# A graph network on one core: where batch norm stands in the first batch of three convolutions

## The chip, the cores and the metric

The kernel runs on one core of one Trainium2 chip. The metric is the device time of one execution in microseconds, lower is better; runs are given by their median. Besides the plain runs there is one profiled execution, whose trace all durations are taken from. The engines are called PE (TensorE, matmuls), DVE (VectorE), ACT (ScalarE), POOL (GpSimd) and SP (SyncE, here a queue for DMAs).

## What is computed

There are 16 graphs (batches) of 1024 nodes with 128 features each, and a symmetric 0/1 adjacency matrix of 1024 x 1024 for every graph. A gated recurrent graph network of four layers comes first. Then four graph convolutions follow, and the change concerns these. Cut to what matters, the reference of the second part is:

```python
h = jnp.maximum(_layernorm(x, axis=-1), 0.0)
for i in range(4):
    h = jnp.einsum('bnm,bmc->bnc', adj, h @ W[i]) + b[i]
    h = jax.nn.relu(h)
    mu = jnp.mean(h, axis=(0, 1))
    var = jnp.mean(jnp.square(h - mu), axis=(0, 1))
    h = gamma[i] * (h - mu) * jax.lax.rsqrt(var + EPS) + beta[i]
return x + h
```

The mean and the variance of batch norm are taken over all nodes of all 16 graphs, so no value of the next layer's input is known before the last graph of this layer is done. Batch norm is one scale and one shift for each feature channel.

In the kernel features lie in the partitions (128) and nodes along the free axis. The last line of a layer is then `h * scale + shift`, with scale and shift of shape 128 x 1.

## The kernel before

There are two paths. `general_path` runs only if a flag shows inputs that a shorter number format can't hold; here it doesn't run. All that follows is in `exact_path`.

The recurrent part (to line 854) writes to DRAM, for each batch, the transposed adjacency matrix in bfloat16 (`adjT_d`), the layer's result (`xmid_d`) and the normed input of the convolutions (`ymid_d`). Its weights are in `w_mT` and `w_hhT`.

The four convolutions (lines 864 to 990) go through the batches one by one. In what follows convolution 1 is the first, with i = 0 in the code, and convolutions 2 to 4 have i = 1 to 3.

- `load_adjT(b, i)` (line 868) loads the eight row blocks of a batch's adjacency matrix from DRAM, 256 KB each, through SP's queue. They land in eight single tiles (`packed`, even batches) or one large tile (`block`, odd batches). ACT (line 876, every third one) or DVE (line 878) widens each to a 128 x 1024 tile `wide`. The tag `row` has twelve buffers: eight for the batch in work and four for the next.
- `conv_input(b, i, aff)` (line 895) applies scale and shift to the features `feat[b]` on ACT (line 897).
- `conv_hw(b, i, hT)` (line 900) multiplies by W on PE (line 493). The product of one batch is split by `features_times` into two parts, a rounded one (ACT, line 495) and the rest (DVE, line 496), so that the fast matmul format loses nothing.
- `aggregate` (line 511) multiplies the adjacency rows by these two parts: for each of eight row blocks j two parts and two halves of the nodes, 32 matmuls of 128 x 512 a batch (line 516), accumulated in two PSUM banks. The banks are `m0`, `m1` in even batches and `g_r`, `g_z` in odd ones (`banks`, line 906). The last batch of convolutions 2 to 4 uses `aggregate_apart` (line 503), which does one half of the nodes after the other.
- `conv_done` (line 909) applies ReLU and the bias on ACT (line 912), puts the result in `feat[b]`, and takes its statistics on DVE (line 913).
- `affine(i, stats)` (line 882) makes scale and shift: one aggregation of the statistics on DVE (885), a square root on ACT (888), and four small DVE operations (889 to 892).

In convolution 1 there is no batch norm in front. There the kernel aggregates first (`first_split`, line 916, splits the input) and multiplies by W behind it: `first_weights` (line 924) copies the two PSUM halves to SBUF and multiplies by W in `g_hn`, `g_xn` (line 931). It does that for batch b in the middle of the aggregation of batch b+1, and for the last batch after everything else.

In convolutions 2 to 4 the product with W of batch b+1 is written ahead of the aggregation of batch b. Batch 0's normalization and product stand ahead of the loop over batches, and so behind the last batch of the layer before:

```python
    for i in range(1, L):
        stats = small.tile([P, B * NH, 6], F32, tag="bn_st", name=f"stats{i}")
        hw = conv_hw(0, i, conv_input(0, i, aff))
        for b in range(B):
            rows = load_adjT(b, i)
            hw_next = conv_hw(b + 1, i, conv_input(b + 1, i, aff)) if b + 1 < B else None
```

After the fourth convolution the result is scaled and shifted, turned back, added to `xmid_d`'s values and written (lines 993 to 1004).

In the recurrent part the order of some or all queues is written out by hand (`manual_schedule`). In the convolutions it isn't: the framework makes each engine's order when the program is built, from the order of the source and its own estimate of when operands are ready. On the chip each engine then runs its own instructions in that fixed order, and waits for the others through semaphores.

Of the kernel before, what the change touches and what calls it, by code (L numbers as in the profile page):

```python
# [8 lines left out]
F32 = mybir.dt.float32  # L9
F32R = mybir.dt.float32r  # L10
# [3 lines left out]
AF = mybir.ActivationFunctionType  # L14
ALU = mybir.AluOpType
AX = mybir.AxisListType
P = 128
HALF = 512
# [323 lines left out]
def exact_path(  # L342
# [21 lines left out]
    nc = tc.nc  # L364
    B, N, C = x.shape
    L = g_weight.shape[0]
    NB = N // P
    NH = N // HALF
    BH = HALF // P
# [9 lines left out]
    def acc(tag, name):  # L379
        return ps_m.tile([P, HALF], F32, tag=tag, name=name)  # L380

    def tmp(name):
        return ps_t.tile([P, HALF], F32, tag="tmp", name=name)
# [8 lines left out]
    def row_tile(name):  # L392
        return keep.tile([P, N], F32R, tag="row", name=name, bufs=12)

    def half_tile(name):
        return keep.tile([P, N], BF16, tag="half", name=name, bufs=8)

    def turned_tile(name):
        return keep.tile([P, NB, N], BF16, tag="adjT", name=name, bufs=1)

    def hw_tiles(b, name):
        return [keep.tile([P, N], F32R, tag=f"hw{b % 2}{s}", name=f"{name}_{s}") for s in range(2)]
# [6 lines left out]
    ones = const.tile([P, 1], F32, tag="ones", name="ones")  # L409
# [3 lines left out]
    w_c = const.tile([P, L, C], F32, tag="w_c", name="w_c")  # L413
    w_mT = const.tile([P, L, 3 * C], F32, tag="w_mT", name="w_mT")
# [12 lines left out]
    def cvec(kind, i):  # L427
        o = 6 * L + kind * L + i
        return vecs[:, o : o + 1]
# [54 lines left out]
    def features_times(w, hT, hw, g, name):  # L484

        pt = tmp(f"hw_{name}_{g}")
        for q in range(BH):
            j = g * BH + q
            src = hT[:, j * P : (j + 1) * P]
            if w is None:  # L490
                nc.tensor.transpose(pt[:, q * P : (q + 1) * P], src, ident)  # L491
            else:
                nc.tensor.matmul(pt[:, q * P : (q + 1) * P], src, w, start=True, stop=True)  # L493
        cols = slice(g * HALF, (g + 1) * HALF)
        nc.scalar.copy(hw[0][:, cols], pt)  # L495
        nc.vector.tensor_sub(hw[1][:, cols], pt, hw[0][:, cols].bitcast(F32))  # L496

    def aggregate_apart(pm, hw, rows):

        for hf in range(NH):  # L500
            for j in range(NB):
                for s in range(2):
                    nc.tensor.matmul(  # L503
                        pm[hf],
                        hw[s][:, j * P : (j + 1) * P],
                        rows[j][:, hf * HALF : (hf + 1) * HALF],
                        start=(j == 0 and s == 0),
                        stop=(j == NB - 1 and s == 1),
                    )

    def aggregate(pm, hw, rows, g):
        for q in range(BH):
            j = g * BH + q
            for s in range(2):
                for hf in range(NH):
                    nc.tensor.matmul(  # L516
                        pm[hf],
                        hw[s][:, j * P : (j + 1) * P],
                        rows[j][:, hf * HALF : (hf + 1) * HALF],
                        start=(j == 0 and s == 0),  # L520
                        stop=(j == NB - 1 and s == 1),
                    )


    with ExitStack() as st:
        work = st.enter_context(tc.tile_pool(name="work", bufs=2))
# [338 lines left out]
    work = ctx.enter_context(tc.tile_pool(name="work2", bufs=2))  # L865
    feat = [feat_pool.tile([P, N], F32, tag=f"f{b}", name=f"feat{b}") for b in range(B)]

    def load_adjT(b, i):
        ts = []
        block = turned_tile(f"block{b}_{i}") if b % 2 else None  # L870
        for j in range(NB):
            t = block[:, j, :] if b % 2 else half_tile(f"packed{b}_{i}_{j}")
            nc.sync.dma_start(t, adjT_d[b][:, j, :])
            r = row_tile(f"wide{b}_{i}_{j}")
            if j % 3 == 1:
                nc.scalar.copy(r, t)  # L876
            else:
                nc.vector.tensor_copy(r, t)  # L878
            ts.append(r)
        return ts  # L880

    def affine(i, stats):

        mv = small.tile([P, 2], F32, tag="bn_mv", name=f"bn_mv{i}")
        nc.vector.bn_aggr(mv, stats.rearrange("p k s -> p (k s)"))
        sc = small.tile([P, 1], F32, tag="bn_sc", name=f"bn_sc{i}")
        sh = small.tile([P, 1], F32, tag="bn_sh", name=f"bn_sh{i}")
        nc.scalar.activation(sc, mv[:, 1:2], AF.Sqrt, bias=eps_t)
        nc.vector.reciprocal(sc, sc)
        nc.vector.tensor_mul(sc, sc, cvec(1, i))  # L890
        nc.vector.tensor_mul(sh, mv[:, 0:1], sc)
        nc.vector.tensor_sub(sh, cvec(2, i), sh)
        return sc, sh

    def conv_input(b, i, aff):
        hT = work.tile([P, N], F32, tag="h", name=f"bn{b}_{i}", bufs=3)
        nc.scalar.activation(hT, feat[b], AF.Identity, bias=aff[1], scale=aff[0])
        return hT

    def conv_hw(b, i, hT):  # L900
        hw = hw_tiles(b, f"chw{b}_{i}")
        for g in range(NH):
            features_times(w_c[:, i, :], hT, hw, g, f"c{b}_{i}")
        return hw

    def banks(b, i):
        return [acc(t, f"pc{b}_{i}_{t}") for t in (("m0", "m1") if b % 2 == 0 else ("g_r", "g_z"))]

    def conv_done(b, i, pm, stats):
        for hf in range(NH):  # L910
            dst = feat[b][:, hf * HALF : (hf + 1) * HALF]
            last = nc.scalar.activation(dst, pm[hf], AF.Relu, bias=cvec(0, i))
            nc.vector.bn_stats(stats[:, b * NH + hf, :], dst)
        return last

    def first_split(b):
        yt = flat(f"y{b}").rearrange("p k c -> p (k c)")
        nc.gpsimd.dma_start(yt, ymid_d[b])
        hw = hw_tiles(b, f"chw{b}_0")
        nc.scalar.copy(hw[0], yt)  # L920
        nc.vector.tensor_sub(hw[1], yt, hw[0].bitcast(F32))
        return hw

    def first_weights(b, pm, stats):

        mt = work.tile([P, N], F32, tag="h", name=f"cm{b}", bufs=3)
        pc = [acc(t, f"pw{b}_{t}") for t in ("g_hn", "g_xn")]
        for hf in range(NH):
            cols = slice(hf * HALF, (hf + 1) * HALF)
            nc.scalar.copy(mt[:, cols], pm[hf])  # L930
            nc.tensor.matmul(pc[hf], w_c[:, 0, :], mt[:, cols], start=True, stop=True)  # L931
        return conv_done(b, 0, pc, stats)

    xo = []

    def by_node(d, hf):
        return d.rearrange("(k p) c -> p k c", p=P)[:, hf * BH : (hf + 1) * BH, :]

    def fetch_x(b):
# [13 lines left out]
        for k in range(0 if b == 2 else 4, len(xo)):  # L953
            for hf in range(NH):
                nc.gpsimd.dma_start(xo[k][hf].rearrange("p (k c) -> p k c", c=C), by_node(xmid_d[k], hf))

    stats = small.tile([P, B * NH, 6], F32, tag="bn_st", name="stats0")
    hw, waiting = first_split(0), None
    for b in range(B):
        rows = load_adjT(b, 0)  # L960
        hw_next = first_split(b + 1) if b + 1 < B else None
        pm = banks(b, 0)
        aggregate(pm, hw, rows, 0)
        if waiting:
            last = first_weights(*waiting, stats)
            if b == 1:
                with tc.issue_after(last.ins):
                    sb.rest()
        aggregate(pm, hw, rows, 1)
        hw, waiting = hw_next, (b, pm)  # L970
    first_weights(*waiting, stats)
    aff = affine(0, stats)

    for i in range(1, L):
        stats = small.tile([P, B * NH, 6], F32, tag="bn_st", name=f"stats{i}")
        hw = conv_hw(0, i, conv_input(0, i, aff))
        for b in range(B):
            rows = load_adjT(b, i)
            hw_next = conv_hw(b + 1, i, conv_input(b + 1, i, aff)) if b + 1 < B else None
            if i == L - 1:  # L980
                fetch_x(b)
            pm = banks(b, i)
            if b + 1 < B:
                for g in range(NH):
                    aggregate(pm, hw, rows, g)
            else:
                aggregate_apart(pm, hw, rows)
            conv_done(b, i, pm, stats)
            hw = hw_next
        aff = affine(i, stats)  # L990


    turns = ["tmp", "tmp", "m0", "m1", "g_r", "g_z", "g_hn", "g_xn"]
    for b in range(B):
        hT = conv_input(b, L, aff)
        for hf in range(NH):
            tag = turns[(b * NH + hf) % len(turns)]
            pt = tmp(f"pt_o{b}_{hf}") if tag == "tmp" else acc(tag, f"pt_o{b}_{hf}")
            for q in range(BH):
                k = hf * BH + q  # L1000
# [56 lines left out]
```

## Time and profile before

| what | value |
|---|---|
| median of 3 runs | 1886.74 us (1886.47 to 1887.95) |
| profiled execution, its own time | 1884.96 us |
| span of its trace (first to last instruction) | 1883.2 us |
| mean granted PE clock | 0.986 |
| aggregation in the recurrent part (line 516, `pm`) | 2048 matmuls, 403 ns each |
| aggregation in even batches of the convolutions (line 516, `pc_m`) | 1024 matmuls, 396 ns each |
| h·W of convolutions 2 to 4 (line 493) | 768 instructions, 286 ns each |
| normalization of 128 x 1024 (line 897) | 64, 1239 ns each |
| widening of one row block | DVE 160 + 160, 693 ns; ACT 96 + 96, 1048 ns |
| load of one row block, issue to landing | 5.3 to 5.7 us (median) |

How to read it. Times are in microseconds from the first instruction of the trace. Matmuls are pipelined, so one of 396 ns doesn't hold the engine for as long; the distance between the starts of two is the time that it costs. `PEld` is the load of the weights, which runs beside the matmuls. An fp32 matmul on `w_c` appears as two instructions in the trace. A row such as `[5.07 <-ACT bn L897]` says that the engine stood idle for 5.07 us before this instruction and that what ended the idleness was an operation `bn` of ACT, line 897. The clock is given as a share of full speed.

### The profile page before, as it was taken

How to read it: one execution, taken by the hardware profiler on the slowest of the kernel's cores; microseconds unless marked ns; L12 is line 12 of the kernel's file. 1: busy time of each engine (PE TensorE's matmuls, PEld its weight loads, DVE VectorE, ACT ScalarE, POOL GpSimd, SP SyncE). 2: the span in 40 equal slices, each digit the busy share in tenths (PEclk: the TensorE clock that was granted, in tenths of full speed). 3: DMA queues.
4: the chain of work that ended last, by engine and by line, in shares of the span. 5: the costliest groups of instructions: out<-in, count | busy, mean ns of one | idle time of the engine just before them, and what ended most of it. 6: DMA issues, size and time to landing. Idle time of an engine off the chain costs nothing.

```text
span 1883.2 us, 21902 instructions
## 1 busy us (share of the span) xinstructions
PE 1826.3 (97%) x7324; PEld 1259.9 (67%) x7324; DVE 1209.0 (64%) x2235; ACT 1041.8 (55%) x1561; POOL 287.5 (15%) x369
## 2 busy tenths in 40 slices
PE   7999999999999999999999999999989989989995
PEld 4666656666656566656665666667768878878884
DVE  5746864865784685595586476576656656665664
ACT  4354563563545454445456353476767767767764
POOL 3130230231141032033023012010100000000021
PEclk8999999999999999999999999999999999999997
DMA  7487476385386476557547536269956757675768
GB/s 258 120 229 255 157 203 216 140 223 170 134 256 189 147 190 202 200 168 234 190 157 203 208 114 169 85 220 319 305 187 214 246 179 246 223 247 180 250 208 259
DMA packets 267824, 381.21 MB, mean 202 GB/s; under 512 B 149716, under 2 KB 171896, under 8 KB 263864
## 3 DMA queue, kind: packets, MB, share of 16 engines
q1 hardware_dynamic: 250032, 246.21, 43.2%
q0 software_dynamic: 17456, 133.45, 20.2%
q8 instruction: 59, 0.97, 0.2%
q14 instruction: 61, 0.50, 0.1%
q10 hardware_dynamic: 216, 0.08, 0.0%
HBM read 287.39 MB, written 117.44 MB: 215 GB/s over the span
## 4 chain that ended last, share of the span: by engine, by line
PE 44%; issue 5%; DMA 3%; DVE 2%; POOL 1%; ACT 1%; SPq 0%; DVEq 0%; POOLq 0%; ACTq 0%
PE pc_m L516 12%; PE pc_g_r L516 5%; PE pc_g_z L516 5%; PE pm L516 5%; PE hw_c L493 5%; PE g_z L720 2%; PE g_r L720 2%; DMA adjT<-half 2%; PE g_xn L720 1%; PE g_hn L720 1%; PE pt_o L1001 1%; PE pw_g_hn L931 1%; PE pw_g_xn L931 1%; PE pc_g_r L503 1%; PE hw_g L491 0%
## 5 line engine op out<-in xcount | busy, mean ns | idle before, releaser
L516 PE MATMUL pm<-row,ghw 128*128 128x512 f32 x2048 | 505.0, 403 | 1.7 <-ACT ghw L697 1.7
L516 PEld LDWEIGHTS pm<-row,ghw 128*128 128x128 f32 x2048 | 383.4, 188 | 107.0 <-issue 31.6
L516 PE MATMUL pc_m<-wide,chw 128*128 128x512 f32 x1024 | 247.6, 396 | 0.0
L516 PEld LDWEIGHTS pc_m<-wide,chw 128*128 128x128 f32 x1024 | 190.7, 189 | 41.5 <-issue 3.8
L733 ACT ACTIVATE r<-r,vecs 128x512 f32<-128x512 f32 x128 | 92.3, 721 | 203.5 <-DVE r L732 203.4
L516 PE MATMUL pc_g_r<-wide,chw 128*128 128x512 f32 x464 | 185.8, 400 | 0.0
L516 PE MATMUL pc_g_z<-wide,chw 128*128 128x512 f32 x464 | 180.8, 390 | 0.0
L575 POOL CAST half<-row 128x1024 bf16<-128x1024 f32 x128 | 139.9, 1109 | 248.8 <-DMA adjT<-half 167.8
L878 DVE CAST wide<-packed 128x1024 fp32r<-128x1024 bf16 x160 | 110.5, 694 | 81.9 <-PE pc_m L516 62.4
L878 DVE CAST wide<-block 128x1024 fp32r<-128x1024 bf16 x160 | 110.4, 693 | 80.0 <-PE pc_g_z L516 42.2
L734 ACT ACTIVATE z<-g_z,brz 128x512 f32<-128x512 f32 x128 | 87.4, 683 | 121.5 <-PE g_z L720 121.5
L496 DVE TENSOR_TENSOR ghw<-hw_g,ghw 128x512 fp32r<-128x512 f32 x96 | 61.7, 683 | 122.7 <-ACT ghw L495 122.7
L720 PE MATMUL g_xn<-m,w_mT 128*128 128x512 f32 x256 | 131.7, 596 | 3.9 <-DVE r L732 3.9
L876 ACT CAST wide<-packed 128x1024 fp32r<-128x1024 bf16 x96 | 100.6, 1048 | 60.7 <-PE pc_g_z L516 30.1
L876 ACT CAST wide<-block 128x1024 fp32r<-128x1024 bf16 x96 | 100.6, 1048 | 60.2 <-PE pc_m L516 34.0
L720 PE MATMUL g_r<-m,w_mT 128*128 128x512 f32 x256 | 131.2, 594 | 0.0
L570 DVE TENSOR_REDUCE low<-row 128x1 f32<-128x1024 uint16 x112 | 130.9, 1201 | 0.0
L720 PE MATMUL g_z<-m,w_mT 128*128 128x512 f32 x256 | 130.7, 592 | 0.0
L730 ACT ACTIVATE r<-g_r,brz 128x512 f32<-128x512 f32 x128 | 87.8, 686 | 61.1 <-PE g_r L720 60.0
L736 DVE TENSOR_TENSOR h<-h,r 128x512 f32<-128x512 f32 x96 | 69.6, 725 | 78.7 <-ACT r L733 78.7
L731 DVE SCALAR_TENSOR_TENSOR r<-g_hn,vecs,r 128x512 f32<-128x512 f32 x128 | 95.1, 743 | 36.4 <-PE g_hn L720 19.1
L708 ACT COPY m<-pm 128x512 f32<-128x512 f32 x128 | 68.1, 583 | 89.4 <-PE pm L516 89.4
(128 smaller groups left out, 2767.8 us busy)
## 6 DMA issues: line engine op xcount, KB each, us to landing
packed<-adjT_d SPq DMA_DIRECT2D x256, 256.0 KB, 5.7
block<-adjT_d SPq DMA_DIRECT2D x256, 256.0 KB, 5.3
raw<-in_adj_dram POOLq DMA_DIRECT2D x112, 512.0 KB, 11.6
row<-raw SPq DMA_DIRECT2D x112, 512.0 KB, 6.1
adjT_d<-adjT POOLq DMA_DIRECT2D x16, 2048.0 KB, 7.2
xmid_d<-x POOLq DMA_DIRECT2D x16, 512.0 KB, 4.1
y<-ymid_d POOLq DMA_DIRECT2D x16, 512.0 KB, 6.1
xo<-xmid_d POOLq DMA_DIRECT2D x32, 256.0 KB, 6.4
```

The costliest lines, as they stand in the source:

```text
L493: nc.tensor.matmul(pt[:, q * P : (q + 1) * P], src, w, start=True, stop=True)
L516: nc.tensor.matmul(pm[hf], hw[s][:, j * P : (j + 1) * P], rows[j][:, hf * HALF : (hf + 1) * HALF], start=(j == 0 and s == 0), stop=(j == N ...
L570: nc.vector.tensor_reduce(low[:, k : k + 1], lows, axis=AX.X, op=ALU.max)
L575: nc.gpsimd.tensor_copy(t, row.bitcast(F32))
L720: nc.tensor.matmul(po, wT[:, i, g * C : (g + 1) * C], rhs, start=start, stop=stop)
L730: nc.scalar.activation(r, pr, AF.Sigmoid, bias=brz[:, 3 * i : 3 * i + 1])
L731: nc.vector.scalar_tensor_tensor(r, phn, b_hn(i), r, ALU.add, ALU.mult)
L733: nc.scalar.activation(r, r, AF.Tanh, bias=b_in(i))
L734: self.last_act = nc.scalar.activation(z, pz, AF.Sigmoid, bias=brz[:, 3 * i + 1 : 3 * i + 2])
L736: nc.vector.tensor_sub(ho, hin, r)
L876: nc.scalar.copy(r, t)
L878: nc.vector.tensor_copy(r, t)
```

## The change

A convolution `adj @ ((h*scale + shift) @ W)` equals `((adj @ h)*scale + degree*shift) @ W`, where degree is the row sum of the adjacency matrix. The change uses this for batch 0 of convolutions 2 to 4: its features are split and aggregated as they are, and scale, shift times degree, and W come behind. The other fifteen batches stay as they were.

- `raw_split(i)` transposes `feat[0]` and splits it. It stands ahead of the last batch's aggregation in the convolution before.
- At the start of a convolution batch 0's rows 0 and 1 are aggregated, then (convolution 2 only) the W step of convolution 1's last batch follows, then `affine`, rows 2 to 5, batch 1's normalization in two halves with its product with W, and rows 6 and 7.
- `raw_weights(i, ...)` stands in the middle of batch 1's aggregation: for each half one scaled copy on ACT, one multiply-add on DVE, and a matmul by W into `g_hn`, `g_xn`; then ReLU and statistics.
- `row_sums(rows)` makes the degree once, in convolution 1 behind the aggregation of batch 0, with 16 matmuls on a tile of ones, and keeps it in the space of `w_mT`.

```diff
     def aggregate(pm, hw, rows, g):
-        for q in range(BH):
-            j = g * BH + q
+        aggregate_rows(pm, hw, rows, range(g * BH, (g + 1) * BH))
+
+    def aggregate_rows(pm, hw, rows, js):
+        for j in js:
             for s in range(2):
                 for hf in range(NH):
                     nc.tensor.matmul(
...
-    def conv_input(b, i, aff):
+    def conv_input(b, i, aff, parts=1):
         hT = work.tile([P, N], F32, tag="h", name=f"bn{b}_{i}", bufs=3)
-        nc.scalar.activation(hT, feat[b], AF.Identity, bias=aff[1], scale=aff[0])
+        for k in range(parts):
+            cols = slice(k * N // parts, (k + 1) * N // parts)
+            nc.scalar.activation(hT[:, cols], feat[b][:, cols], AF.Identity, bias=aff[1], scale=aff[0])
         return hT
...
+    def raw_split(i):
+
+        hw = hw_tiles(0, f"chw0_{i}")
+        for g in range(NH):
+            features_times(None, feat[0], hw, g, f"c0_{i}")
+        return hw
+
+    def raw_weights(i, pm, aff, stats):
+
+        mt = work.tile([P, N], F32, tag="h", name=f"cr{i}", bufs=3)
+        pc = [acc(t, f"pr{i}_{t}") for t in ("g_hn", "g_xn")]
+        for hf in range(NH):
+            cols = slice(hf * HALF, (hf + 1) * HALF)
+            nc.scalar.activation(mt[:, cols], pm[hf], AF.Copy, scale=aff[0])
+            nc.vector.scalar_tensor_tensor(mt[:, cols], degree[:, cols], aff[1], mt[:, cols], ALU.mult, ALU.add)
+            nc.tensor.matmul(pc[hf], w_c[:, i, :], mt[:, cols], start=True, stop=True)
+        conv_done(0, i, pc, stats)
+
+    def row_sums(rows):
+
+        pd = [tmp(f"pt_deg{hf}") for hf in range(NH)]
+        for j in range(NB):
+            for hf in range(NH):
+                nc.tensor.matmul(
+                    pd[hf], ones_r, rows[j][:, hf * HALF : (hf + 1) * HALF], start=(j == 0), stop=(j == NB - 1)
+                )
+        for hf in range(NH):
+            nc.scalar.copy(degree[:, hf * HALF : (hf + 1) * HALF], pd[hf])
...
+    ones_r = work.tile([P, P], F32R, tag="ones_r", name="ones_r", bufs=1)
+    nc.vector.tensor_copy(ones_r, ones.to_broadcast([P, P]))
+    degree = w_mT.rearrange("p l c -> p (l c)")[:, :N]
+
...
+        if b == B - 1:
+            hw_next = raw_split(1)
         aggregate(pm, hw, rows, 1)
+        if b == 0:
+            row_sums(rows)
         hw, waiting = hw_next, (b, pm)
-    first_weights(*waiting, stats)
-    aff = affine(0, stats)
+
+
 
     for i in range(1, L):
+        rows, pm0, hw0 = load_adjT(0, i), banks(0, i), hw
+        aggregate_rows(pm0, hw0, rows, range(2))
+        if i == 1:
+            first_weights(*waiting, stats)
+        aff = affine(i - 1, stats)
         stats = small.tile([P, B * NH, 6], F32, tag="bn_st", name=f"stats{i}")
-        hw = conv_hw(0, i, conv_input(0, i, aff))
-        for b in range(B):
+        aggregate_rows(pm0, hw0, rows, range(2, 6))
+        hw = conv_hw(1, i, conv_input(1, i, aff, 2))
+        aggregate_rows(pm0, hw0, rows, range(6, NB))
+        for b in range(1, B):
             rows = load_adjT(b, i)
-            hw_next = conv_hw(b + 1, i, conv_input(b + 1, i, aff)) if b + 1 < B else None
+            if b + 1 < B:
+                hw_next = conv_hw(b + 1, i, conv_input(b + 1, i, aff))
+            elif i + 1 < L:
+                hw_next = raw_split(i + 1)
             if i == L - 1:
                 fetch_x(b)
             pm = banks(b, i)
             if b + 1 < B:
-                for g in range(NH):
-                    aggregate(pm, hw, rows, g)
+                aggregate(pm, hw, rows, 0)
+                if b == 1:
+                    raw_weights(i, pm0, aff, stats)
+                aggregate(pm, hw, rows, 1)
             else:
                 aggregate_apart(pm, hw, rows)
             conv_done(b, i, pm, stats)
             hw = hw_next
-        aff = affine(i, stats)
+    aff = affine(L - 1, stats)
```

## The prediction

> **What bounds the kernel now.** I read the page first (busy shares, 40 slices), then the three places where one convolution ends and the next begins in the timeline, then windows with the granted clock, and last the chain of waits around those places.
>
> ```profile
> span 1883.2 us, 21902 instructions
> PE 1826.3 (97%) x7324; PEld 1259.9 (67%) x7324; DVE 1209.0 (64%) x2235; ACT 1041.8 (55%) x1561; POOL 287.5 (15%) x369
> ```
>
> PE is busy in 97% of the span; DVE and ACT have a third or more to spare. So a microsecond of PE work costs a microsecond, and a microsecond of PE idleness is one to be won. Inside a convolution there is none; three PE lines of convolution 2 show its period:
>
> ```profile
> 1600.43 1.95 PE L493 MATMUL hw_c<-w_c,bn 128*128 128x128 f32 x16
> 1602.13 7.51 PE L516 MATMUL pc_m<-wide,chw 128*128 128x512 f32 x32
> 1609.48 1.95 PE L493 MATMUL hw_c<-w_c,bn 128*128 128x128 f32 x16
> ```
>
> Columns: start, duration, engine, line, operation. A batch is 1.70 us of h·W (1602.13 - 1600.43) and 7.35 us of aggregation, 9.05 us start to start, with nothing between. At the end of a convolution it stops. The chain there, and the timeline's PE lines:
>
> ```profile
> 1537.69 0.70 DVE stats L913
> ...
> 1538.42 1.03 DVE bn_mv L885
> ...
> 1539.47 0.30 ACT bn_sc L888
> ...
> 1540.58 1.25 ACT bn L897
> ...
> 1541.88 3.78 PE hw_c L493 x16
> ```
>
> ```profile
> 1533.02 3.79 PE L503 MATMUL pc_g_z<-wide,chw 128*128 128x512 f32 x16
> 1541.88 3.78 PE L493 MATMUL hw_c<-w_c,bn 128*128 128x128 f32 x16 [5.07 <-ACT bn L897]
> ```
>
> PE ends at 1536.81 (1533.02 + 3.79) and begins at 1541.88: 5.07 us for ReLU, statistics, the chain of small operations and one normalization. The 16 h·W matmuls then take 3.78 us, not 1.95. The windows say why; their columns are the window, its length, busy us of PE, PEld, DVE, ACT, POOL, then the granted PE clock, DMA share and GB/s:
>
> ```profile
> 1392.00:1394.00 2.00, 2.00 (x13) 1.87 (x13) 0.69 (x1) 1.24 (x3) 0.00 (x0) 0.72 0.00 0
> ...
> 1400.00:1530.00 130.00, 130.00 (x688) 111.81 (x687) 84.01 (x129) 90.19 (x113) 0.00 (x0) 1.00 0.69 230
> ...
> 1540.00:1546.00 6.00, 4.12 (x18) 4.03 (x19) 1.17 (x4) 4.35 (x5) 0.00 (x0) 0.50 0.06 19
> 1546.00:1548.00 2.00, 2.00 (x15) 1.91 (x14) 0.69 (x1) 1.97 (x3) 0.00 (x0) 0.82 0.00 0
> ...
> 1700.00:1702.00 2.00, 2.00 (x14) 1.86 (x14) 0.69 (x1) 0.83 (x2) 0.00 (x0) 0.92 0.00 0
> ```
>
> After the pause PE runs at half clock. From the partial windows: until about 1393.1, 1546.7 and 1700.3.
>
> **What a seam costs, twice.** Directly: PE waits 5.01 us at the first seam (1385.22 to 1390.23) and 5.07 at each of the others, 15.15 together. At half clock it works 2.9, 4.85 and 5.9 us (from 1390.23, 1541.88, 1694.39) and loses half of that, 6.8. Sum 22.0. By difference: PE's work on convolutions 2, 3, 4 ends at 1536.81, 1689.32 and 1842.34, the one before at 1385.22, so they take 151.6, 152.5 and 153.0; sixteen dense batches are 144.8 each; the excess is 22.7. I use 22.7. The first seam has 0.75 more: convolution 1's last aggregation ends at 1382.74 and its W matmuls at 1385.22, 2.48 us for work that costs 1.73 (below), because PE waits for the ACT copy.
>
> **The Trainium skill.** "TensorE: Matmul & The Clock Gate", Part 1: an idle window of some 3.4 us puts the array at half clock and a busy one restores it. The trace agrees: 5 us gaps, clock 0.50. The same page, "Step-by-step: what each phase is for": matmuls stay in program order, only weight loads are pulled ahead; so one waiting h·W matmul in PE's queue holds everything behind it. The trace doesn't test that alone. "ScalarE: Activation LUTs", "What ACT_TABLE_LOAD costs": an ACTIVATE is 186 ns + 0.833 ns per element, each per-partition operand 93 ns more. That gives 1.22 us for L897 (measured 1.24), so as estimates from that page 0.80 us for the half normalization and 0.71 for the scaled copy of 512 columns, which the trace doesn't have.
>
> **What the change adds on PE.** Prices from these lines:
>
> ```profile
> 1115.93 1.03 PE L491 MATMUL hw_g<-ident,h 128*128 128x128 f32 x8
> 1116.81 1.02 PE L720 MATMUL g_r<-h_in,w_hhT 128*128 128x512 f32 x2
> ```
>
> Eight transposes hold PE 0.88 us (1116.81 - 1115.93). Two W matmuls on 512 columns appear as four instructions, and in convolution 1 the aggregation matmul behind such a step ends at 1379.30 (start 1378.50 + 0.80) instead of 1377.57 (1377.18, where its turn would have been, + 0.39): 1.73 us. An aggregation matmul repeats every 0.2266 us.
> - Row sums, once, behind batch 0 of convolution 1: 16 matmuls of the aggregation's shape and type, 16 x 0.2266 = 3.63. PE is full there (124.5 of 125.2 us in 1260 to 1385.2), so all counts. Two ACT copies (0.58 each) hide: ACT is busy 88 of these 125 us. The rows of batch 0 are held 3.6 us longer; the next batch has four rows ahead in the 12 buffers and gets one back every 0.45 us.
> - Batch 0's W step: 1.73 instead of h·W's 1.70, plus raw split's 0.88: 0.91 per convolution, 2.7 for three. The raw split stands ahead of the last batch's aggregation, as the next batch's h·W did.
> - ACT loses one normalization and gains two scaled copies; DVE gains two operations like L736 (0.73 us). Both have room over 9.05 us (a batch is on ACT three casts of 1.05, one normalization of 1.25, two copies of 0.59 and two ReLUs of 0.69, 7.0 together; on DVE five casts, two statistics and two subtractions of 0.69, 6.2). The ones tile is once, under the recurrent part.
> - No DMA is added; the loads keep their order on SP's queue, and POOL's queue is not passed by any moved step. DMA share in dense stretches is 0.69, so losing the pauses doesn't starve it.
>
> Together 3.63 + 2.7 = 6.4 us added against 22.7 + 0.75 = 23.4 that can go: 17.0 at best.
>
> **What stays of the seams.** The cover is batch 0's aggregation, whose rows and halves depend on no batch norm: rows 0 to 5 are 24 matmuls, 5.44 us, rows 6 and 7 another 1.81 behind batch 1's h·W. The chain at seams 2 and 3 takes 3.77 us to the normalization (1536.81 to 1540.58), 0.80 for its first half: 4.6, under 5.44. At seam 1 the first 8 matmuls (1.81) cover the ACT copy before the W step; after it 16 (3.63) stand against 3.72 + 0.80 = 4.5: 0.9 us of idleness, too short for a half clock. Batch 1's casts stand in the same ACT and DVE queues: one (1.05 on ACT, 0.69 on DVE) caught in the chain makes it 6.3 and leaves 0.9 at a seam. The new waits: batch 0's W step in the middle of batch 1 waits for a scaled copy and a multiply-add, with batch 1's second half queued behind it. The bank was complete half a batch earlier, so it waits only if ACT is late; 0 to 1 us each. Next on the path after the seam is PE itself. I take 0.9 + 2 x 0.4 for the seams and 0.3 per W step, 2.6 in all; bounds 0 and 7.
>
> So 17.0 - 2.6 = 14.4 us. The profiled execution took 1884.96 us (span 1883.2) and becomes about 1870.6; the runs' median lies 1.8 above it, so 1886.74 becomes 1872.3; I say **1872**.
>
> **Rivals.**
> 1. Seams mostly close but ACT and DVE queues are in the way: 2 to 3 us stay at each seam or at the W step. For it: after a seam ACT has ReLU, square root, two half normalizations, four copies and casts, about 9 us of work in 9 us plus waiting. Against: half of the next batch's rows are already cast. 17.0 - 8 gives 1878.
> 2. Seams close fully, the W step is free: 1886.74 - 17.0 = 1870.
> 3. Slower: the order on PE's queue, which isn't written by hand in this part, puts batch 1's h·W (waiting for batch norm) ahead of nearly all of batch 0's aggregation. Each seam then keeps pause and half clock, and only the added work remains: 1886.7 + 6.4 - 0.75 = 1892. It decides from 17.0 / 3 = 5.7 us left per seam. For it: in the trace of before, h·W groups and aggregation are mixed after a seam (16 h·W, 1 aggregation, 8 h·W, 2 aggregations). Against: these followed readiness, and batch 0's aggregation is ready before the seam.
> 4. Row sums at four passes (as the W step) instead of one: 16 x 0.86 = 13.8 in place of 3.6, 1882. The operands have the type of L516's, so this is unlikely.
>
> **Numbers.** Forecast (1870.5 to 1876) 0.52; rival 2, 0.17; rival 1, 0.16; rival 3, 0.10, of which 0.01 so weak that it is no change; rival 4 or a mixture, 0.05, of which 0.04 within no change. A measurement tells about 0.2%, 3.8 us, from no change. Range: from a microsecond or two below the best case, 1868, to 1880, which takes in rival 1 and the bound of 7 (1876.7). Faster 0.86, same 0.05, slower 0.09.
>
> **What would show it.** Right: windows around the three seams keep clock 1.00; no PE wait over 1 us for L897; convolutions 2 to 4 take 146 to 147.5 us each; PE has four matmuls more in all (12 of the W step, 16 of the row sums, 24 transposes, 48 of h·W fewer); convolution 1 is 3.6 longer. Wrong: a PE gap over 3 us at a seam with clock 0.50; a wait of the aggregation on L878 or L876 casts after a seam; a wait of the W step on ACT over 1 us; conv 1 longer by more than 5 us; the recurrent part changed.

## The result, and the profile after

| | before | after |
|---|---|---|
| median | 1886.61 us (4 runs, 1885.69 to 1887.95) | 1870.50 us (4 runs, 1869.83 to 1872.78) |
| profiled execution | 1884.96 us, span 1883.2 | 1870.41 us, span 1868.6 |
| mean granted PE clock | 0.986 | 0.991 |

The ratio of the medians is 0.9912, with a 95% interval of 0.990 to 0.9925: 16.1 us less. The forecast was 1872.0 with a range of 1868 to 1880.

The page of after begins so (busy us, share of the span, instructions):

```profile
span 1868.6 us, 21940 instructions
PE 1827.9 (98%) x7328; PEld 1257.9 (67%) x7328; DVE 1215.2 (65%) x2242; ACT 1041.8 (56%) x1569; POOL 287.8 (15%) x369
```

PE has four matmuls more, as forecast, and is busy 1.6 us longer in a span that is 14.6 us shorter, so its idle time fell from 56.9 to 40.7 us. (Work at half clock counts as busy in these sums.) Lines of the kernel have moved: from 516 on they stand two further down, from 897 on four and at the end more. The aggregation is now L518, the normalization L901, ReLU L916.

To see where, I cut each trace at PE's first matmul of the convolutions and at the end of the last aggregation of each. "Conv 2" thus holds the seam in front of it.

| us | first matmul | conv 1 | conv 2 | conv 3 | conv 4 | rest |
|---|---|---|---|---|---|---|
| before | 1237.39 | 145.35 | 154.07 | 152.51 | 153.02 | 40.86 |
| after | 1239.39 | 149.29 | 148.70 | 145.84 | 144.95 | 40.43 |
| difference | +2.00 | +3.94 | -5.37 | -6.67 | -8.07 | -0.43 |

The first column is the recurrent part, in which nothing of PE's work was changed. It differs from run to run: with the same code it lay between 1236.90 and 1241.82 in nine profiles. Convolutions 1 to 4 agree within 0.2 us between profiles that have the same code there; the rest lay between 40.4 and 41.7 in all of them. Without the first column the differences sum to -16.6, of which the convolutions are -16.2, beside the 16.1 of the medians.

The seam between convolutions 2 and 3, PE's rows of the timeline of after (start, duration, engine, line, operation):

```profile
1533.59 3.79 PE L503 MATMUL pc_g_z<-wide,chw 128*128 128x512 f32 x16
1537.21 5.83 PE L518 MATMUL pc_m<-wide,chw 128*128 128x512 f32 x25
1542.90 2.05 PE L493 MATMUL hw_c<-w_c,bn 128*128 128x128 f32 x16
1544.71 1.85 PE L518 MATMUL pc_m<-wide,chw 128*128 128x512 f32 x7
1546.39 1.95 PE L493 MATMUL hw_c<-w_c,bn 128*128 128x128 f32 x16
```

Where before stood a pause of 5.07 us and then 3.78 us of product, batch 0's aggregation now begins while the last one drains, and the product takes 2.05. No row has an idle time. What goes on meanwhile on ACT:

```profile
1537.50 0.68 ACT L916 ACTIVATE feat<-pc_g_z,vecs 128x512 f32<-128x512 f32 x1
1538.36 1.05 ACT L878 CAST wide<-block 128x1024 fp32r<-128x1024 bf16 x1 [0.18 <-ACT feat L916]
1540.00 0.30 ACT L890 ACTIVATE bn_sc<-bn_mv,eps_t 128x1 f32<-128x1 f32 x1 [0.59 <-DVE bn_mv L887]
1541.08 1.05 ACT L878 CAST wide<-block 128x1024 fp32r<-128x1024 bf16 x1 [0.79 <-DMA packed<-adjT_d]
1542.04 2.65 ACT L901 ACTIVATE bn<-feat,bn_sh,bn_sc 128x512 f32<-128x512 f32 x3
```

The chain from ReLU to batch 1's product is still there, and is longer than before: from 1537.38, where the last aggregation ends, to 1542.90 are 5.52 us (before 5.07). Up to the square root nothing has changed (2.62 us, before 2.66). From the square root's start to the normalization's are 2.04 us (before 1.11): a cast of batch 1's rows (the widening to `wide`) stands in it on ACT (1541.08), and on DVE another, between the small operations:

```profile
1540.61 0.16 DVE L892 TENSOR_TENSOR bn_sc<-bn_sc,vecs 128x1 f32<-128x1 f32 x1
1540.69 0.69 DVE L880 CAST wide<-block 128x1024 fp32r<-128x1024 bf16 x1
1541.30 0.15 DVE L893 TENSOR_TENSOR bn_sh<-bn_mv,bn_sc 128x1 f32<-128x1 f32 x1
```

From the normalization to the product it is 0.86 us, less than before (1.30), because only the first half has to be done. The 25 matmuls ahead of the product end at about 1542.87 (1537.21 + 25 x 0.2266), so the cover (the work that PE has meanwhile) just suffices.

The windows of after, at the three seams (window, length, busy us of PE, PEld, DVE, ACT, POOL, granted clock, DMA share, GB/s):

```profile
1386.00:1402.00 16.00, 15.66 (x75) 11.99 (x74) 10.78 (x21) 11.92 (x17) 0.00 (x0) 1.00 0.55 179
1537.00:1549.00 12.00, 12.00 (x70) 10.37 (x69) 9.05 (x18) 10.44 (x15) 0.00 (x0) 1.00 0.74 246
1683.00:1695.00 12.00, 12.00 (x70) 10.34 (x70) 9.05 (x18) 10.44 (x15) 0.00 (x0) 1.00 0.76 248
```

PE is full at the second and third, and the clock is 1.00 at all. The waits of PE from the first convolution to the end (engine, line, what it waited for; us in total, times, longest) were, in before, three at the seams for the normalization, one behind convolution 4, and two for the copy ahead of a W step:

```profile
PE hw_c L493 <- ACT bn L897: 15.1, 3, 5.1
PE pt_o L1001 <- ACT bn L897: 4.9, 1, 4.9
PE pw_g_hn L931 <- ACT cm L930: 1.1, 2, 0.6
```

In after there are two:

```profile
PE pt_o L1054 <- ACT bn L901: 4.9, 1, 4.9
PE pc_g_r L518 <- ACT chw L495: 0.3, 1, 0.3
```

The 4.9 us are those behind convolution 4, which the change doesn't touch; the other is at the first seam:

```profile
1390.34 1.02 PE L935 MATMUL pw_g_hn<-cm,w_c 128*128 128x512 f32 x2
1391.20 1.02 PE L935 MATMUL pw_g_xn<-cm,w_c 128*128 128x512 f32 x2
1391.66 6.05 PE L518 MATMUL pc_m<-wide,chw 128*128 128x512 f32 x24
1397.79 2.05 PE L493 MATMUL hw_c<-w_c,bn 128*128 128x128 f32 x16
1400.10 0.51 PE L518 MATMUL pc_g_r<-wide,chw 128*128 128x512 f32 x1 [0.25 <-ACT chw L495]
```

The source writes 16 matmuls of batch 0 between convolution 1's last W step and batch 1's product. The framework put all 24 that were left there.

### The profile page after: what moved, and what is told of

Read it like the earlier page. It is cut to its first block, busy times and chain, and to the rows that moved or that the text cites. A ratio compares the mean times of both kernels' runs of the same rounds, so it can differ in the third digit from the quotient of the medians.

```text
span 1868.6 us, 21940 instructions
## 1 busy us (share of the span) xinstructions
PE 1827.9 (98%) x7328; PEld 1257.9 (67%) x7328; DVE 1215.2 (65%) x2242; ACT 1041.8 (56%) x1569; POOL 287.8 (15%) x369
## 4 chain that ended last, share of the span: by engine, by line
PE 42%; issue 5%; DVE 3%; DMA 3%; POOL 1%; ACT 1%; SPq 0%; DVEq 0%; POOLq 0%; ACTq 0%
PE pc_m L518 12%; PE pc_g_z L518 6%; PE pc_g_r L518 6%; PE pm L518 4%; PE hw_c L493 4%; PE g_z L722 2%; PE g_r L722 2%; DMA adjT<-half 2%; DVE low L572 1%; PE g_xn L722 1%; PE pt_o L1054 1%; PE g_hn L722 1%; PE pw_g_hn L935 1%; PE pw_g_xn L935 1%; PE pc_g_r L503 1%
## 5 line engine op out<-in xcount | busy, mean ns | idle before, releaser
L518 PE MATMUL pm<-row,ghw 128*128 128x512 f32 x2048 | 506.7, 404 | 2.1 <-ACT ghw L699 2.1
L518 PEld LDWEIGHTS pm<-row,ghw 128*128 128x128 f32 x2048 | 385.0, 189 | 107.4 <-issue 31.9
L518 PE MATMUL pc_m<-wide,chw 128*128 128x512 f32 x1024 | 246.1, 396 | 0.0
L518 PEld LDWEIGHTS pc_m<-wide,chw 128*128 128x128 f32 x1024 | 190.6, 188 | 42.2 <-issue 4.3
L518 PE MATMUL pc_g_r<-wide,chw 128*128 128x512 f32 x464 | 187.2, 404 | 0.3 <-ACT chw L495 0.3
L518 PE MATMUL pc_g_z<-wide,chw 128*128 128x512 f32 x464 | 181.3, 391 | 0.0
```

The costliest lines, as they stand in the source:

```text
L518: nc.tensor.matmul(pm[hf], hw[s][:, j * P : (j + 1) * P], rows[j][:, hf * HALF : (hf + 1) * HALF], start=(j == 0 and s == 0), stop=(j == N ...
```

## The experiments

Each has a short diff, against the changed kernel if nothing else is said. Times are medians; ratios are against runs of the kernel before beside it. The readings rest mostly on the stages of the profiled executions, cut as above:

| us | first matmul | conv 1 | conv 2 | conv 3 | conv 4 |
|---|---|---|---|---|---|
| before | 1237.39 | 145.35 | 154.07 | 152.51 | 153.02 |
| 1: before, PE kept busy | 1238.36 | 145.19 | 153.85 | 151.42 | 151.42 |
| 2: the same, copies first | 1240.69 | 145.16 | 152.98 | 150.58 | 150.59 |
| after | 1239.39 | 149.29 | 148.70 | 145.84 | 144.95 |
| 3: product first | 1238.72 | 149.32 | 153.76 | 150.27 | 149.33 |
| 4: half of the cover | 1239.22 | 149.31 | 152.58 | 149.50 | 147.02 |
| 5: normalization in one piece | 1241.82 | 149.30 | 148.63 | 146.19 | 145.32 |
| 6: without row sums | 1236.90 | 146.05 | 148.67 | 145.87 | 144.97 |
| 7: row sums in the opening | 1239.75 | 146.16 | 148.66 | 145.85 | 144.95 |
| 8: after, again | 1238.42 | 149.28 | 148.68 | 145.85 | 144.95 |
| 8: experiment 7, again | 1239.30 | 146.08 | 148.66 | 145.91 | 144.95 |

**1. Before, with PE kept busy in the pauses.** Does the half clock alone cost what the direct sum gave it (6.8 us)? Five matmuls that nobody reads stand behind the last work of each of convolutions 1 to 3 (`mm_last`). The diff is against the kernel before.

```diff
+    def idle_work(i):
+        pt = tmp(f"pt_warm{i}")
+        with tc.issue_after(mm_last[0].ins):
+            for k in range(5):
+                nc.tensor.matmul(pt, ident, w_c.rearrange("p l c -> p (l c)"), start=True, stop=True)
...
     first_weights(*waiting, stats)
+    idle_work(0)
     aff = affine(0, stats)
...
+        if i < L - 1:
+            idle_work(i)
         aff = affine(i, stats)
```

> The kernel before, with five matmuls of 128 x 512 (identity on the W matrices, result unused, 0.86 us each by the two-instruction W step of the trace) behind the last aggregation of convolutions 1 to 3, so that PE is busy in the pause and has nothing useful to do. Theory (a seam costs 5 us of waiting and about 2.3 us of half clock): the waiting stays, the half clock goes; no clock of 0.50 at the three seams, time 1886.6 - 6.8 = 1879.8. Rival (the first products after a pause are slow because two PSUM buffers wait for ACT and DVE, the clock only comes with it): the same as before within 1 us, 1886.

Measured: 1884.13 (21 runs), ratio 0.9985 (0.9978 to 0.9992), 3.3 us less than before, where 6.8 was expected. The clock is 1.00 at all three seams. PE's timeline at the second:

```profile
1537.24 4.45 PE L940 MATMUL pt_warm<-w_c,ident 128*128 128x512 f32 x10
1542.46 2.05 PE L493 MATMUL hw_c<-w_c,bn 128*128 128x128 f32 x16 [0.77 <-ACT bn L899]
1545.20 0.73 PE L518 MATMUL pc_m<-wide,chw 128*128 128x512 f32 x2 [0.68 <-ACT chw L495]
```

and ACT's:

```profile
1541.17 3.50 ACT L899 ACTIVATE bn<-feat,bn_sh,bn_sc 128x1024 f32<-128x1024 f32 x3 [0.81 <-DVE bn_sh L894]
1544.58 1.05 ACT L495 CAST chw<-hw_c 128x512 fp32r<-128x512 f32 x2
```

The product is at full speed (2.05, not 3.78), but what it gained is half lost again: ACT does batch 0's normalization and two more in a row (3.50 us) before it copies batch 0's product, and PE waits 0.68 us for that copy. In before, where the product is slow, no such wait is recorded. By stages the clock was worth 0.22, 1.09 and 1.60 us, 2.9 in all; the first of these is hardly more than the scatter.

**2. The same, with ACT's copies ahead of batch 1's normalization.** Is the second wait the queue on ACT? `act_last` is the last copy of batch 0's product; the diff is against experiment 1.

```diff
-            hw_next = conv_hw(b + 1, i, conv_input(b + 1, i, aff)) if b + 1 < B else None
+            if b == 0:
+                with tc.issue_after(act_last[0].ins):
+                    hT = conv_input(1, i, aff)
+                hw_next = conv_hw(1, i, hT)
...
```

> As e1_before_kept_busy (the kernel before, PE kept busy in the pauses), and batch 1's normalization is queued on ACT behind the copies of batch 0's product instead of ahead of them. Theory (at full clock PE next waits for those copies, 0.7 us at each seam, because two more normalizations of 1.25 us stand ahead of them on ACT; this had hidden part of the half clock): that wait goes, convolutions 2 to 4 become 0.5 to 1.5 us shorter each than in e1_before_kept_busy, 1880 to 1883. Rival (the copies wait for something else): stages as in e1_before_kept_busy.

Measured: 1881.97 (7 runs), ratio 0.9971 (0.9960 to 0.9983). The stages are 0.87, 0.84 and 0.83 us shorter than in the first experiment, and the row behind the product has lost its wait:

```profile
1543.90 2.05 PE L493 MATMUL hw_c<-w_c,bn 128*128 128x128 f32 x16 [0.78 <-ACT bn L899]
1545.79 2.38 PE L518 MATMUL pc_m<-wide,chw 128*128 128x512 f32 x8
```

So a seam of before came to 7.5 to 8.2 us (its stage above a dense one of 144.8, for conv 2 also above the W step's 1.73). Clock and copies together, which the two experiments take away, are 1.1 us in conv 2, 1.9 in conv 3 and 2.4 in conv 4. The rest, 5.8 to 6.5, is the wait for batch norm itself and what goes with starting again.

**3. The product first.** Batch 1's product is put ahead of rows 2 to 7 of batch 0 on PE's queue (`mm_last` is its last matmul). This is the order of rival 3.

```diff
-        aggregate_rows(pm0, hw0, rows, range(2, 6))
+        aggregate_rows(pm0, hw0, rows, range(2, 2))
         hw = conv_hw(1, i, conv_input(1, i, aff, 2))
-        aggregate_rows(pm0, hw0, rows, range(6, NB))
+        with tc.issue_after(mm_last[0].ins):
+            aggregate_rows(pm0, hw0, rows, range(2, NB))
```

> The changed kernel with batch 1's product with W forced ahead of batch 0's rows 2 to 7 on PE's queue: same work, but only rows 0 and 1 stand ahead of the instruction that waits for batch norm. Theory (batch 0's aggregation is the cover): PE waits 3.5 to 4.5 us at each seam again, about 12 in all, and half clock comes back at some of them, 0 to 3 us each: 1882 to 1890. Rival (the gain comes from what is no longer in the chain, batch 0's normalization and product, not from the cover): 1870 to 1873.

Measured: 1886.74 (13 runs), ratio 0.9995 (0.9987 to 1.0003). By the medians the whole gain is gone. PE's timeline at the second seam:

```profile
1541.64 1.98 PE L520 MATMUL pc_m<-wide,chw 128*128 128x512 f32 x8
1546.48 3.43 PE L493 MATMUL hw_c<-w_c,bn 128*128 128x128 f32 x16 [2.87 <-ACT bn L903]
```

and its waits:

```profile
PE hw_c L493 <- ACT bn L903: 10.3, 3, 4.6
```

The three waits are 4.58, 2.87 and 2.87 us, and behind each the clock is 0.50 for a while (1396 to 1399, 1546.5 to 1549 and 1697.2 to 1699.2). Behind the second, a somewhat wider window:

```profile
1546.00:1550.00 4.00, 3.52 (x18) 3.48 (x19) 0.69 (x1) 2.90 (x5) 0.00 (x0) 0.58 0.00 0
```

Convolutions 2 to 4 take 5.06, 4.43 and 4.38 us more than in after, 13.9 us together, of the 16.2 by which the four convolutions of after had become shorter. The work is the same; only its place on the queue differs.

The chain is shorter here than in after. ACT's rows of it:

```profile
1544.43 0.30 ACT L892 ACTIVATE bn_sc<-bn_mv,eps_t 128x1 f32<-128x1 f32 x1 [0.59 <-DVE bn_mv L889]
1545.62 2.65 ACT L903 ACTIVATE bn<-feat,bn_sh,bn_sc 128x512 f32<-128x512 f32 x3 [0.90 <-DVE bn_sh L896]
```

No cast stands between the square root and the normalization. From one to the other are 1.19 us, and from the end of the last aggregation (1541.80) to the product 4.68.

**4. Half of the cover.** As experiment 3, with rows 0 to 3 ahead of the product and 4 to 7 behind it (`range(2, 4)`, `range(4, NB)`).

> As e3_product_first, but with rows 0 to 3 ahead of batch 1's product and rows 4 to 7 behind it. Theory (the wait is the chain minus the matmuls ahead of it on PE's queue, and half clock returns only behind a wait of some 2.9 us and more): the chain was 4.7 us there, 16 matmuls cover 3.6, so about 1.05 us of waiting at the seams of convolutions 3 and 4 and no half clock; at the first seam 8 of the 16 lie behind the W step, so 4.58 - 1.81 = 2.8 us and perhaps half clock. In all 5 to 7 us more than the changed kernel: 1876 to 1878. Rival (the order around the product costs, not the cover): about as slow as e3_product_first, 1883 and more.

Measured: 1881.78 (8 runs), ratio 0.9972 (0.9961 to 0.9982), a miss by 4 us. PE's timeline at the second and the third seam:

```profile
1540.95 3.79 PE L520 MATMUL pc_m<-wide,chw 128*128 128x512 f32 x16
1546.63 2.49 PE L493 MATMUL hw_c<-w_c,bn 128*128 128x128 f32 x16 [1.90 <-ACT bn L903]
...
1696.13 2.05 PE L493 MATMUL hw_c<-w_c,bn 128*128 128x128 f32 x16 [1.90 <-ACT bn L903]
```

I had worked with experiment 3's chain of 4.7 us and so a pause of 1.1. The chain was 5.52 (1541.11 to 1546.63), with a cast on ACT and one on DVE in it as in after, and the pause 1.90. And the windows behind the same pause differ in the clock:

```profile
1546.00:1552.00 6.00, 5.37 (x25) 4.71 (x26) 2.08 (x3) 3.47 (x5) 0.00 (x0) 0.72 0.77 223
1696.00:1702.00 6.00, 5.87 (x35) 5.20 (x36) 2.69 (x5) 4.25 (x7) 0.00 (x0) 1.00 0.89 250
```

Conv 3 lost 3.66 us against after, conv 4 only 2.07. The difference of 1.6 us is as much as the largest of the three prices of the half clock in experiment 1. At the first seam, which isn't shown, the pause was 3.18 us and conv 2 lost 3.88.

**5. The normalization in one piece.** `conv_input(1, i, aff)` in place of `conv_input(1, i, aff, 2)`: is the split into halves needed?

> The changed kernel with batch 1's normalization in one instruction of 1024 columns instead of two of 512. Theory (in the changed kernel the 25 matmuls ahead of the product end within 0.1 us of the first half's end at the seams of convolutions 3 and 4): the chain is 0.45 us longer, PE waits up to 0.45 us at each of these seams, in all 0.5 to 1.5 us more: 1871.3 to 1872.3, to be read from the stages of the trace. Rival (there is slack left, or the order is chosen anew with more cover): no wait of PE, same stages within 0.2 us.

Measured: 1872.73 (4 runs), ratio 0.9919 (0.9903 to 0.9936). Conv 3 and conv 4 are 0.36 us longer, conv 2 is 0.07 shorter although PE waits 0.51 us there. At the second and third seam there is no wait at all: from the normalization to the product it is now 1.30 us in place of 0.86, and the framework chose a new order, with 27 matmuls ahead of the product in place of 25 (2 x 0.2266 = 0.45). What makes these two stages longer without a wait isn't shown. The convolutions hold 0.65 us of the difference from after; most of the rest lies in the recurrent part, which in the profiled execution was at the long end of its scatter (1241.82). So the halves are worth little, because the order adapts to the chain.

**6. Without the row sums.** The two lines `if b == 0: row_sums(rows)` go; the degree is then left uncomputed.

> The changed kernel without the row sums: the degree isn't computed, and what stands in its space is used in its place. Theory (PE has no room in convolution 1, all of the 16 matmuls count): 3.7 us less than the changed kernel, 1866.8. Rival (the row sums lie in time in which PE would wait for casts or loads): 1870 to 1870.5.

Measured: 1868.18 (4 runs), ratio 0.9901 (0.9886 to 0.9916), 1.4 us above what was expected. The stage says more than the median: conv 1 goes from 149.29 to 146.05, so the row sums cost 3.24 us there, where 3.63 was counted.

**7. The row sums in an earlier pause.** In the opening of the program (here of after) PE waits for a long time:

```profile
27.00 1.97 PE L613 MATMUL pt_in<-ident,y_in 128*128 128x128 f32 x8 [5.29 <-DVE vecs L448]
```

Batch 0's rows are in SBUF there in the recurrent part's format. The row sums are taken from them, behind the first aggregation, and kept in one byte per value until DVE widens them. One byte holds sums up to 255; the inputs here have an edge with a probability of some 0.008, so a row of the matrix has about 9 ones (an estimate). As the matrix is symmetric the column sums serve. (`row_sums` and the tile of ones also move to the front of the program.)

```diff
             sa.agg_step(1)
+            row_sums(sa.rows)
             turn_small(*small_in)
...
     def row_sums(rows):
-        pd = [tmp(f"pt_deg{hf}") for hf in range(NH)]
+        pd = [acc(t, f"pt_deg_{t}") for t in ("g_hn", "g_xn")]
...
-            nc.scalar.copy(degree[:, hf * HALF : (hf + 1) * HALF], pd[hf])
+            nc.scalar.copy(deg8[:, hf * HALF : (hf + 1) * HALF], pd[hf])
...
         if b == B - 1:
+            nc.vector.tensor_copy(degree, deg8)
             hw_next = raw_split(1)
         aggregate(pm, hw, rows, 1)
-        if b == 0:
-            row_sums(rows)
```

> The changed kernel with the row sums of batch 0 moved to the opening, behind the first aggregation, where PE stood idle for 5.3 us before the transposes of line 613; it sums the columns, which is the same for a symmetric matrix, keeps them in 8 bits and widens them on DVE in convolution 1. Theory: 3.7 us leave convolution 1 and hide in the opening, 1866.8, or less if the busier PE gets its full clock earlier. Rival (the opening's order on ACT, which also has the two copies now, makes the opening 1 to 4 us longer): 1868 to 1871.

Measured: 1867.55 (4 runs), ratio 0.9892 (0.9877 to 0.9907). Conv 1 is back at 146.16. The window of the opening, in after:

```profile
20.00:28.00 8.00, 2.71 (x13) 2.01 (x12) 7.31 (x10) 1.07 (x2) 3.22 (x4) 0.73 0.97 329
```

and here:

```profile
20.00:28.00 8.00, 6.99 (x32) 5.15 (x30) 7.96 (x9) 2.53 (x5) 3.13 (x3) 1.00 0.92 316
```

PE does 4.28 us more in the same 8 us, and the first matmul of the gates starts at 37.30 us (37.41 in after). In the second pair of profiles, of experiment 8, it is 38.81 against 38.15. The first matmul of the convolutions comes 0.4 and 0.9 us later in the two pairs, which is within the scatter of the recurrent part. So most of the 3.2 us is saved; that the row sums are wholly free there isn't shown.

**8. The changed kernel and experiment 7 once more,** since 2.95 us between two medians is little.

> The changed kernel once more, unchanged, beside e9_degree_in_opening_again on the same chip. Every theory: 0.9912 of the kernel before, about 1870.5.

> The kernel of e4_degree_in_opening once more, to have more runs of it. Theory: 3 us below the changed kernel, 0.9892 of the kernel before. Rival (the first runs were lucky in the recurrent part): within 1 us of the changed kernel, 0.991.

Measured: 1870.42 (0.9910, 0.9894 to 0.9927) and 1867.80 (0.9900, 0.9883 to 0.9916), each 4 runs. The two ran on different chips, each beside the kernel before. By these ratios the second is 1.9 us faster, less than expected, and the intervals overlap; by the medians it is 2.6. What decides is conv 1, which is 3.2 us shorter (3.1 in the first pair). This version is the fastest that was measured.

## Why the prediction was right, step by step

- **What the seams could give (23.4 us).** Right in sum. The stages of before stand 7.5, 7.7 and 8.2 us above dense ones, 23.5 together. The direct split into a wait of 15.2 and 6.8 of half clock doesn't say what each is worth alone, though. Taken away alone, half clock was worth 2.9 us (experiment 1), because a wait for ACT's copies came forward once it was gone (experiment 2). The forecast didn't suffer from this, since the change takes both away together, and its two sums (22.0 and 22.7) differ little.
- **Row sums (3.63).** Right that all of it counts; it measured 3.24 (experiment 6). That it would be 13.8 (rival 4) is excluded.
- **W step and raw split (0.91 a convolution).** Right. The raw split in conv 1 is 0.70 (experiment 6's 146.05 against 145.35; 0.89 against the 145.16 of experiment 2, which has before's code there), and conv 3, with raw split and W step, is 145.84 where 144.8 + 0.03 + 0.88 gives 145.71. No wait of the W step on ACT or DVE was seen.
- **The cover.** Right that batch 0's aggregation is what pays: with only a quarter of it ahead of the product next to nothing is won (experiment 3). But the chain was put at 4.6 us against a cover of 5.44, and it is 5.52: the case that the prediction named, casts of batch 1's rows caught in the chain, is what happens at both later seams, and the 0.93 us between square root and normalization is the whole difference. Experiments 3 and 4 bear it out: with the same two casts in it the chain is 5.52, without them 4.68. It cost nothing because the 0.8 us that was counted as spare took most of it, and because the order has 25 matmuls ahead of the product and not the 24 that the source writes; nothing is spare now. That the order came out so was luck, as far as the prediction goes.
- **The residual (2.6 taken).** This is the term that was mis-sized: about 1.5. Above dense stages (with raw split and W step) conv 2 keeps 1.3 us and conv 3 and 4 0.1 each, where 0.9 + 0.3, 0.4 + 0.3 and 0.4 + 0.3 were taken. The 0.9 us of idleness at the first seam didn't come, because two errors met there: the chain behind the W step is 5.57 us (1392.22 to 1397.79) and not 4.5, but 24 matmuls (5.44 us) stand ahead of the product instead of 16 (3.63). With 16 it would have been about 2 us (an estimate from these figures). Of conv 2's 1.3 us one wait of 0.25 is on record; the rest lies around the product and in the rows behind it, where product and aggregation alternate in small groups, and what causes it isn't shown. The 0.4 and 0.3 at each later place were allowances for collisions that cost nothing. So conv 3 and 4 lie below the 146 to 147.5 us that were named as a sign of being right; conv 2, without the W step's 1.73, is 147.0.
- **The sum.** 23.5 - 3.24 - 2.55 (0.70 + 2 x 0.88 + 3 x 0.03) - 1.5 = 16.2, and the rest of the program was 0.4 us shorter: 16.6 by the stages. Predicted 14.4. Against the 16.2 the misses all lie on one side: 0.1 in the seams, 0.6 in the added work, 1.1 in the residual. So of the named cases rival 2 (1870) was the closest in number, and its picture of the second and third seams is the right one; the forecast was 1.5 us above. That the own time of the profiled run (1870.4) hit the forecast of 1870.6 is chance: its recurrent part was 2.0 us longer than that of before.
- **The Trainium skill.** "ScalarE: Activation LUTs" gave 0.71 us for the scaled copy and 0.80 for the half normalization; the six of each took 0.687 and 0.806 on average. "TensorE: Matmul & The Clock Gate", on matmuls in program order, fits what experiment 3 shows: PE stands for 2.87 us with batch 0's matmuls, which need no batch norm, behind the waiting one.

Not tried: a version with the full cover and the casts kept out of the chain, which would show whether the cover then has a microsecond to spare.

## What to carry to other kernels

In this kernel a reduction over all graphs stopped PE, which bounds it, between two layers. What covered the pause was work of the next layer that commutes with the normalization, and it did so only where it stood ahead of the dependent work on PE's queue. Size a pause by its whole stage against a dense one; what one part of it is worth alone shows only when that part is taken away (2.9 us here, where 6.8 was counted), since another wait may come forward. And work that is needed once can go into a pause that exists already: it cost 3.2 us in a full stage, and in the opening no more than the scatter.

## What was not expected of the hardware

The clock fell after pauses much shorter than those of before (5 us). A pause of 2.87 us gave half clock at both later seams of experiment 3, and one of 1.90 us at one seam of experiment 4 but not at the next, with the same 16 matmuls ahead of it. The Trainium skill ("TensorE: Matmul & The Clock Gate", Part 1, "What's actually happening") says that activity is watched in windows of 3.4 us that run freely, so that the moment at which a change comes varies. Two different outcomes of one pause would go with that. But the same section has the clock fall after at least one idle window, as the prediction took it, and both pauses are shorter than a window; here the measurement decides, and what sets the clock back after 1.90 us stays open. The page's advice to keep pauses under some 3 us ("Why this matters for your kernels") is too generous for these runs, in which the half clock behind a pause of 1.90 us went with 1.6 us more.
